# Shared-expert products in sixes instead of twelves through the last unit of cross-attention

## The chip, the cores and the metric

The kernel runs on one core of one Trainium2 chip. The metric is the device time of one execution, in microseconds (us), lower being better. Engines are named as the profile names them: PE (matrix multiply; PEld is its weight load), DVE (vector), ACT (activation), POOL, and SP, which issues most of the loads. TensorE's granted clock is given as a share of full speed.

## The reference, cut to what matters

One pre-norm decoder layer on `x` of 16 sequences by 64 tokens by 256 features (1024 tokens), all in float32:

```
x = x + self_attention(layernorm(x))          # 16 heads, weights as 4-bit codes times scales
x = x + cross_attention(layernorm(x), ctx)    # 16 heads, context of 64 rows by 64
x = x + moe(layernorm(x))

def moe(xt):                                  # 16 experts of inner width 176, plus shared experts of 352
    scores  = softmax(xt @ Wg.T)              # the 4 best of 16 experts, out of the 2 best groups of 4
    y       = sum over chosen experts of w_e * (silu(xt @ W1_e.T) * (xt @ W3_e.T)) @ W2_e.T
    z       = (silu(xt @ Ws1.T) * (xt @ Ws3.T)) @ Ws2.T
    return y + z
```

In cross-attention each head's normalized scores are multiplied with the context, then projected back to 256 features and added to `x`. The products `xt @ Ws1.T` and `xt @ Ws3.T` are the "shared up products" of this document.

## The kernel before, in words

Tokens lie on the 128 partitions in eight tiles of 128 (`x[0]` to `x[7]`), handled as two halves of 512 tokens. A float32 product is made from two rounded parts of each operand, a high and a low one: `three` lists the three part products, so that a 256-deep product of one tile is six matmuls. `parts_of` (L111) makes the parts: ACT copies the high part, DVE subtracts to get the low one (both rows stand under L112 and L113).

Cross-attention runs in eight units, each four heads (a "quad") of one half. In turn n of the loop the unit n is rotated, unit n-1 is scored and unit n-2 finished. To finish a unit means: `transposed` (L352) turns the normalized scores `pn` on PE, ACT copies the result into `pt` in two rows (L360, L361), `pair_context` (L1070) multiplies `pt` with the context into PSUM tile `av`, `parts_of` turns `av` into `c_t`, and `cross_project` (L1095 for its additions) projects four tiles of 128 tokens with 24 matmuls and lets DVE add them to `x`. Each unit has two pairs of heads, so two `pn`, two `pt`, two `c_t`.

Turn 9 finishes the last unit, of the second half of the tokens. Nothing of cross-attention is left to be mixed in, so the shared up products of the first half (`normed[0]`, ready since turn 6) stand there: six products of six matmuls, called in pairs by `shared_up` (two products and the Silu on ACT, L937), each followed by `shared_hidden` (DVE multiplies gate and up, L948, and splits the result in parts) and later by `shared_output` (36 matmuls, additions L970).

After the last projection the second half is normalized (`layernorm_t(3, (1,))`: statistics on DVE, one power on POOL L177, two rows of ACT L199 and two of DVE L192), turned on PE (L216), and routed by `choose(1)`: 16 small matmuls with the router's weights, a long run of small DVE instructions (L791 to L856), and in their midst two matmuls L819 and L820 for the places in the experts' lists. Its last row (L856) gives the targets of the 16 indirect transfers by which POOL scatters the tokens to the experts (`send`, L864). The experts' loop loads its inputs `xr` from there (L1311).

The builder's scheduler decides the order within each engine from estimated times. `after(...)` (a wrapper of `tc.issue_after`) is the author's way to hold an instruction's place behind another one in that order; it adds no wait on the chip. PSUM has four `mm` tiles, two `at` and two `av`. SP loads the last expert's weights in two pieces (`dense_weights`: `w_last_up`, `w_last_down`), and then the weights of the experts 0 and 1 (L277), which wait until the last `pn` has been computed.

Of the kernel before, what the change touches and what calls it, by code (L numbers as in the profile page):

```python
# [44 lines left out]
SHI = 2 * INTER  # L45
# [26 lines left out]
def decoder_layer(ctx: ExitStack, tc: tile.TileContext, a: dict, out: bass.AP):  # L72
    nc = tc.nc
# [11 lines left out]
    def mm_tile(rows=128, cols=512):  # L85
        return ps_mm.tile([128, 512], F32, tag="mm", name="mm")[:rows, :cols]
# [15 lines left out]
    def matmuls(ps, pairs):  # L102
        for n, (l, r) in enumerate(pairs):
            m = nc.tensor.matmul(ps, lhsT=l, rhs=r, start=(n == 0), stop=(n == len(pairs) - 1))  # L104
        return m.ins

    def three(left, right):

        return [(left[0], right[0]), (left[0], right[1]), (left[1], right[0])]

    def parts_of(src, hi, lo, eng=None):  # L111
        nc.scalar.copy(hi, src)  # L112
        return (eng or nc.vector).tensor_tensor(lo, src, hi, ALU.subtract).ins  # L113


    x_pairs = [acts.tile([128, 2, D], F32, tag=f"x{n}", name=f"x{n}") for n in range(NI // 2)]
# [198 lines left out]
    with ExitStack() as attn:  # L315
# [603 lines left out]
            nc.vector.tensor_reduce(w, ch, AX.X, ALU.add)  # L919
            return w, last, p  # L920

        def shared_up(half, k, pool):

            n = min(128, SHI - k * 128)
            cols = slice(k * 128, k * 128 + n)
            ps = []
            for w in range(2):
                t = mm_tile(rows=n)
                pairs = []
                for c in range(2):  # L930
                    pairs += three(
                        [p[:, w, c, cols] for p in ws13_p], [p[:, c, :] for p in normed[half]]
                    )
# [3 lines left out]
            silus.append(nc.scalar.activation(g, ps[0], AF.Silu).ins)  # L937
# [43 lines left out]
        with (  # L981
# [179 lines left out]
            for n in range(len(units) + 2):  # L1161
# [7 lines left out]
                with after(*([projected] if n < len(units) and projected else [])):  # L1169
                    pts_n = [transposed(pn) for pn in pns.pop(n - 2, ())]  # L1170
                if n < len(units):
                    roped_done = list(roped_last)
                    order = [m for m in [next(rotate, None)] if m]
                    if n - 1 in here:
                        with after(*order, *([pn_turned[0]] if n > 2 else [])):
                            q_rs, product = pair_queries(
                                weights[units[n - 1][0]][1], roped.pop(n - 1), roped_done
                            )
                        order = [product]
                    c_ts = []  # L1180
                    for pt in pts_n:
                        with after(*order):
                            c_t, product = pair_context(pt, units[n - 2][1])
                        order = [product]
                        c_ts.append(c_t)
                    if n == 0:
                        with tc.issue_after(highs[-1]), tc.issue_after(lows[-1]):
                            xn_t += layernorm_t(2, (1,))
                    else:
                        pns[n - 1] = []  # L1190
                        for q_r in q_rs:
                            with after(*order):
                                pn, product = pair_scores(q_r, units[n - 1][1], nc.gpsimd)
                            order = [product]
                            pns[n - 1].append(pn)
                    if n in late:
                        with after(*order):
                            next(prep)
                    with after(*order):
                        next(rotate)  # L1200
                    if n in late:
                        next(prep)
                else:
                    if n - 1 in here:
                        q_rs, _ = pair_queries(weights[units[n - 1][0]][1], roped.pop(n - 1))
                    c_ts = [pair_context(pt, units[n - 2][1])[0] for pt in pts_n]
                    if n - 1 in here:

                        pns[n - 1] = [pair_scores(q_rs[0], units[n - 1][1], nc.vector)[0]]
                    if n - 1 in here:  # L1210
                        pns[n - 1].append(pair_scores(q_rs[1], units[n - 1][1], nc.vector)[0])
                if n - 2 in here:
                    projected = cross_project(
                        weights[units[n - 2][0]][2], c_ts, units[n - 2][1], n - 1 == len(units)
                    )
                for _ in rotate:
                    pass

# [23 lines left out]
                    choose(0)  # L1242
                    send(0, (0, 1))
                if n == 8:
                    w_last = dense_weights()
                    with after(exps[-1]):
                        routed.append(weights_of_choices(0))
                if n == 9:
                    rows[1] = [
                        xw.tile([128, 3, 2, 2, DC], F32, tag="w_s", name="rows1")  # L1250
                        .rearrange("p a b c d -> p (a b c d)")[:, : 2 * ROW]
                        .rearrange("p (a b) -> p a b", a=2)
                        for _ in range(2)
                    ]
                    normed[1] = layernorm_t(3, (1,), token_rows(1))[0]
                    high = highs[-1]
                    scored, placed, aimed = choose(1)
# [319 lines left out]
```

## Time and profile before

| What | Value |
|---|---|
| Time of four runs | 568.45, 572.49, 566.48, 569.26 us; median 568.85 |
| Profiled execution | 568.07 us; span 566.3 us |
| Mean granted clock of TensorE | 0.978 |
| PE / PEld busy | 528.0 / 446.8 us (93% / 79% of the span) |
| DVE / ACT / POOL busy | 385.2 / 304.1 / 227.6 us |
| Turn 9 on PE (from the last unit's first transposes to the second half's transposes) | 392.4 to 417.7 us |
| Routing of the second half (first router matmul to targets) | 419.1 to 430.8 us |
| Scatter of the second half on POOL | from 431.1 us |

A row of a timeline gives the start in us, the time from the first instruction's start to the last one's end, the engine, the line, the operation, what it writes and reads, the shape and the number of instructions; in brackets stands how long the engine was idle before it and what released it. Rows of PE are pipelined: the next row starts before the last one's end, so a stretch is best measured from start to start.

### The profile page before, as it was taken

Reading aid. Unit: us, or ns where it says so; the run is one execution under the profiler, and the core shown is the slowest. Engines: PE = TensorE matmul, PEld = TensorE weight load, DVE = VectorE, ACT = ScalarE, POOL = GpSimd, SP = SyncE. Lnnn points to the kernel's source line nnn. Section 1 sums busy time; section 2 is a strip of 40 time slices with the busy share of each in tenths; the row PEclk is TensorE's granted clock in tenths of the full one; section 3 lists DMA queues with packets and bytes.
Section 4 is the critical chain, followed back from the end, with each engine's and each line's share of the span. In section 5 each row is a group of like instructions: output and inputs, shape, how many; then the busy total and the mean of one; then the engine's idle time right before and its main releaser. Section 6 shows DMA issues by size and latency. Waiting matters only on the chain.

```text
span 566.3 us, 10815 instructions
## 1 busy us (share of the span) xinstructions
PE 528.0 (93%) x4013; PEld 446.8 (79%) x4013; DVE 385.2 (68%) x863; ACT 304.1 (54%) x764; POOL 227.6 (40%) x213
## 2 busy tenths in 40 slices
PE   7999999999999989999999999999799679999972
PEld 6888898998989865867768678678587579999961
DVE  5465473664745899746566487677477489999877
ACT  3667566585575521534625455456426178777551
POOL 4261500101100017426333364453255716888862
PEclk9999999999999999999999999999899889999985
DMA  8464432823200889280010000102311648677475
GB/s 235 143 163 121 114 116 67 225 93 113 76 1 12 271 226 293 92 251 1 19 54 2 8 0 1 30 2 55 137 61 69 220 168 291 223 254 236 124 266 171
DMA packets 44263, 70.84 MB, mean 125 GB/s; under 512 B 11824, under 2 KB 25232, under 8 KB 44208
## 3 DMA queue, kind: packets, MB, share of 16 engines
q1 hardware_dynamic: 39376, 58.71, 35.4%
q0 software_dynamic: 3696, 10.36, 4.7%
q10 hardware_dynamic: 1136, 1.05, 0.5%
q8 instruction: 33, 0.54, 0.4%
q14 instruction: 22, 0.18, 0.1%
HBM read 48.61 MB, written 21.86 MB: 124 GB/s over the span
## 4 chain that ended last, share of the span: by engine, by line


## 5 line engine op out<-in xcount | busy, mean ns | idle before, releaser
L1014 POOL TENSOR_TENSOR roped<-rt,rt 128x512 f32<-128x512 f32 x48 | 61.8, 1309 | 44.9 <-DVE rt L1006 43.9
L104 PE MATMUL mm<-xn,w_q 128*128 128x512 f32 x288 | 72.3, 402 | 0.5 <-ACT xn L222 0.5
L1006 DVE TENSOR_TENSOR rt<-mm,rope_q 128x512 f32<-128x512 f32 x96 | 60.9, 679 | 11.5 <-PE mm L104 11.1
L104 PEld LDWEIGHTS mm<-xn,w_q 128*128 128x128 f32 x288 | 52.7, 188 | 14.4 <-issue 1.2
L104 PE MATMUL mm<-xs,w 128*128 128x384 f32 x270 | 55.0, 353 | 8.1 <-ACT xs L112 6.9
L1360 POOL DMA_INDIRECT yd<-y,to x45 | 48.1, 1068 | 27.0 <-ACT y L1355 13.4
L104 PEld LDWEIGHTS mm<-xs,w 128*128 128x128 f32 x270 | 48.3, 198 | 9.6 <-ACT xs L112 7.6
L325 DVE TENSOR_REDUCE sm_m<-at 128x8 f32<-128x512 f32 x32 | 21.9, 684 | 47.8 <-PE at L582 47.1
L523 POOL TENSOR_TENSOR wv<-code,scale 128x512 fp32r<-128x512 f32 x7 | 9.5, 1352 | 89.7 <-DMA scale<-in_scales 55.6
L1032 PE MATMUL mm<-roped,w_s 128*64 128x512 f32 x192 | 44.9, 599 | 0.2 <-DVE rt L1006 0.2
L331 ACT ACTIVATE p<-at,sm_m 128x64 f32<-128x64 f32 x128 | 38.1, 346 | 12.7 <-DVE sm_m L329 12.6
L565 ACT ACTIVATE qT<-mm,bqkv 128x512 f32<-128x512 f32 x32 | 21.8, 689 | 33.6 <-PE mm L104 33.6
L360 ACT COPY pt<-at 64x512 f32<-64x512 f32 x32 | 18.6, 581 | 38.7 <-PE at L352 38.7
L104 PE MATMUL av<-w,hp 128*128 128x256 f32 x225 | 35.6, 292 | 1.8 <-ACT y L1355 0.9
L104 PE MATMUL mm<-wv,xn 128*128 128x256 f32 x256 | 36.2, 288 | 0.0
L104 PE MATMUL mm<-wo,o 128*128 128x256 f32 x256 | 34.1, 286 | 2.0 <-DVE x L624 1.8
L343 POOL TENSOR_TENSOR pn<-p,sm_s 128x512 f32<-128x512 f32 x14 | 14.6, 1044 | 50.1 <-DVE sm_s L339 50.1
L104 PEld LDWEIGHTS mm<-wo,o 128*128 128x128 f32 x256 | 31.6, 191 | 3.6 <-DVE x L624 3.1
L104 PE MATMUL mm<-xn,wk 128*128 128x512 f32 x128 | 34.3, 399 | 0.0
L104 PE MATMUL mm<-xn,wq 128*128 128x512 f32 x128 | 33.2, 398 | 0.1
L104 PEld LDWEIGHTS av<-w,hp 128*128 128x128 f32 x225 | 30.7, 191 | 3.0 <-ACT y L1355 1.5
L104 PEld LDWEIGHTS mm<-wv,xn 128*128 128x128 f32 x256 | 32.5, 189 | 0.7
(219 smaller groups left out, 1189.9 us busy)
## 6 DMA issues: line engine op xcount, KB each, us to landing
w<-in_W SPq DMA_DIRECT2D x15, 640.0 KB
code<-in_codes SPq DMA_DIRECT2D x32, 256.0 KB
scale<-in_scales SPq DMA_DIRECT2D x32, 256.0 KB
xr<-xd SPq DMA_DIRECT2D x15, 408.0 KB
xd<-zeros SPq DMA_DIRECT2D x8, 720.0 KB
yd<-zeros SPq DMA_DIRECT2D x8, 512.0 KB
got<-yd SPq DMA_DIRECT2D x16, 256.0 KB
wq<-in_Wq SPq DMA_DIRECT2D x4, 512.0 KB
```

The lines of the kernel that those rows point to most:

```text
L104: m = nc.tensor.matmul(ps, lhsT=l, rhs=r, start=(n == 0), stop=(n == len(pairs) - 1))
L325: nc.vector.tensor_reduce(m, sc, AX.X, ALU.max)
L331: last = nc.scalar.activation(p[:, b], sc[:, b], AF.Exp, bias=m[:, b : b + 1], accum_out=s[:, b : b + 1])
L343: .tensor_tensor(pn, p, s.unsqueeze(2).broadcast_to(shape), ALU.mult)
L360: nc.scalar.copy(pt[:S, :, 0, :], ps[:S])
L523: mults[n] = eng.tensor_tensor(w, *loaded[gr].pop(n), ALU.mult).ins
L565: nc.scalar.activation(qk[which][:, half * 512 : (half + 1) * 512], ps, AF.Identity, bias=bqkv[:, which, h : h + 1],).ins
L1006: factors = nc.vector.tensor_tensor(mt, ps3, rope_table(t, 2 * ab + k), ALU.mult)
L1014: nc.gpsimd.tensor_tensor(r.rearrange("p (b s) -> p b s", s=S), one, two, op)
L1032: nc.tensor.matmul(ps[h // 2][(h % 2) * 64 : (h % 2) * 64 + 64], lhsT=w_s[:, t, blk, ab, :], rhs=roped[2 * t + ab], start=first[h], stop=l ...
L1360: sent = nc.gpsimd.indirect_dma_start(out=yd[: (E - 1) * SLOTS + min(TOPK, E - 1 - e) * NT], out_offset=bass.IndirectOffsetOnAxis(ap=to[:, ...
```

## The change

In turn 9 the finishing of the last unit is written out by hand. A helper `shared_products` makes one product of six matmuls. The order on PE becomes: transposes of the first pair, one product, context of the first pair, transposes of the second pair, one product, context of the second pair, one product, then the whole projection (24 matmuls) in one piece, and the other three products behind it. Before, two products (twelve matmuls) stood in each of the two gaps, and the last two products stood inside the projection. The Silus and what follows them are ordered behind the high part of the second `c_t`. The split of `w_last_down` into parts, which stood ahead of the first `c_t` on ACT, is put behind the second `c_t` on ACT and DVE. The count of instructions on each engine is the same. In the built order the transposes of the second half (L216) come after 18 of the 36 matmuls of `shared_output`, no longer after all, and the first six matmuls of `dense_up` come behind the router's matmuls instead of ahead of them.

```diff
     def parts_of(src, hi, lo, eng=None):
-        nc.scalar.copy(hi, src)
+        high_last[0] = nc.scalar.copy(hi, src).ins
         return (eng or nc.vector).tensor_tensor(lo, src, hi, ALU.subtract).ins
...
-        def shared_up(half, k, pool):
+        def shared_products(half, k, w):
 
             n = min(128, SHI - k * 128)
             cols = slice(k * 128, k * 128 + n)
-            ps = []
-            for w in range(2):
-                t = mm_tile(rows=n)
-                ...
-                matmuls(t, pairs)
-                ps.append(t)
+            t = mm_tile(rows=n)
+            pairs = []
+            for c in range(2):
+                pairs += three([p[:, w, c, cols] for p in ws13_p], [p[:, c, :] for p in normed[half]])
+            return t, matmuls(t, pairs)
+
+        def shared_up(half, k, pool, ps=None):
+
+            n = min(128, SHI - k * 128)
+            ps = ps or [shared_products(half, k, w)[0] for w in range(2)]
...
                     nc.sync.dma_start(out=t, in_=a["W123"][E - 1][:, cols])
-                    parts_of(t, parts[0][:, cols], parts[1][:, cols])
-                return parts
+                    if cols.start == 0:
+                        parts_of(t, parts[0][:, cols], parts[1][:, cols])
+                return parts, lambda: parts_of(t, parts[0][:, cols], parts[1][:, cols])
...
+                if n == len(units) + 1:
+
+                    half, ups, c_ts, order = units[-1][1], [], [], []
+                    for pn in pns.pop(n - 2):
+                        with after(*order):
+                            pt = transposed(pn)
+                        with after(pn_turned[0]):
+                            ps, product = shared_products(0, 0, len(ups))
+                        ups.append(ps)
+                        with after(product):
+                            c_t, product = pair_context(pt, half)
+                        c_ts.append(c_t)
+                        order = [product]
+                    c_high = high_last[0]
+                    with after(product):
+                        ps, product = shared_products(0, 1, 0)
+                    ups.append(ps)
+                    with after(product):
+                        projected = cross_project(weights[units[-1][0]][2], c_ts, half, True)
+                    with after(c_high):
+                        rest_of_last()
+                else:
...
                     for k in range(3):
-                        with after(*pn_turned[(0 if k else 1) :]):
-                            up = shared_up(0, k, xa)
+                        while len(ups) < 2 * k + 2:
+                            with after(projected):
+                                ups.append(shared_products(0, k, len(ups) % 2)[0])
+                        with after(c_high):
+                            up = shared_up(0, k, xa, ups[2 * k : 2 * k + 2])
```

More of the change, by code (lines that the diff above doesn't have):

```diff
@@ L111, in parts_of @@
     def parts_of(src, hi, lo, eng=None):
-        nc.scalar.copy(hi, src)
+        high_last[0] = nc.scalar.copy(hi, src).ins
         return (eng or nc.vector).tensor_tensor(lo, src, hi, ALU.subtract).ins
+    high_last = [None]
     x_pairs = [acts.tile([128, 2, D], F32, tag=f"x{n}", name=f"x{n}") for n in range(NI // 2)]
@@ L920, in weights_of_choices @@
             return w, last, p
-        def shared_up(half, k, pool):
+        def shared_products(half, k, w):
             n = min(128, SHI - k * 128)
             cols = slice(k * 128, k * 128 + n)
-            ps = []
-            for w in range(2):
-                t = mm_tile(rows=n)
[L929 to L933, printed above, removed]
-                matmuls(t, pairs)
-                ps.append(t)
+            t = mm_tile(rows=n)
[6 more added lines that the diff above has]
+            ps = ps or [shared_products(half, k, w)[0] for w in range(2)]
             g = pool.tile([128, 512], F32, tag=f"rt{k % 2}0", name="sg")[:n]
@@ L1168, in decoder_layer @@
                 rotate = iter(rotated_queries(weights[qd][0], half, roped[n]) if n in here else ())
[L1169 to L1178, printed above, removed]
-                        order = [product]
-                    c_ts = []
-                    for pt in pts_n:
-                        with after(*order):
[L1183 to L1188, printed above, removed]
-                    else:
[L1190 to L1215, printed above, removed]
+                if n == len(units) + 1:
[9 more added lines that the diff above has]
+                        c_ts.append(c_t)
+                        order = [product]
+                    c_high = high_last[0]
[7 more added lines that the diff above has]
+                else:
+                    with after(*([projected] if n < len(units) and projected else [])):
+                        pts_n = [transposed(pn) for pn in pns.pop(n - 2, ())]
+                    if n < len(units):
+                        roped_done = list(roped_last)
+                        order = [m for m in [next(rotate, None)] if m]
+                        if n - 1 in here:
+                            with after(*order, *([pn_turned[0]] if n > 2 else [])):
+                                q_rs, product = pair_queries(
+                                    weights[units[n - 1][0]][1], roped.pop(n - 1), roped_done
+                                )
+                            order = [product]
+                        c_ts = []
+                        for pt in pts_n:
+                            with after(*order):
+                                c_t, product = pair_context(pt, units[n - 2][1])
+                            order = [product]
+                            c_ts.append(c_t)
+                        if n == 0:
+                            with tc.issue_after(highs[-1]), tc.issue_after(lows[-1]):
+                                xn_t += layernorm_t(2, (1,))
+                        else:
+                            pns[n - 1] = []
+                            for q_r in q_rs:
+                                with after(*order):
+                                    pn, product = pair_scores(q_r, units[n - 1][1], nc.gpsimd)
+                                order = [product]
+                                pns[n - 1].append(pn)
+                        if n in late:
+                            with after(*order):
+                                next(prep)
+                        with after(*order):
+                            next(rotate)
+                        if n in late:
+                            next(prep)
+                    else:
+                        if n - 1 in here:
+                            q_rs, _ = pair_queries(weights[units[n - 1][0]][1], roped.pop(n - 1))
+                        c_ts = [pair_context(pt, units[n - 2][1])[0] for pt in pts_n]
+                        if n - 1 in here:
+                            pns[n - 1] = [pair_scores(q_rs[0], units[n - 1][1], nc.vector)[0]]
+                        if n - 1 in here:
+                            pns[n - 1].append(pair_scores(q_rs[1], units[n - 1][1], nc.vector)[0])
+                    if n - 2 in here:
+                        projected = cross_project(
+                            weights[units[n - 2][0]][2], c_ts, units[n - 2][1], n - 1 == len(units)
+                        )
@@ L1244, in decoder_layer @@
                 if n == 8:
-                    w_last = dense_weights()
+                    w_last, rest_of_last = dense_weights()
                     with after(exps[-1]):
```

## The prediction

> **What bounds the kernel now.** I read the page first: one engine is nearly always busy, so what counts is where PE stops, and what it waits for there.
>
> ```profile
> span 566.3 us, 10815 instructions
> PE 528.0 (93%) x4013; PEld 446.8 (79%) x4013; DVE 385.2 (68%) x863; ACT 304.1 (54%) x764; POOL 227.6 (40%) x213
> ```
>
> The change touches turn 9 alone, so next comes the timeline of PE there.
>
> ```profile
> 392.73 3.05 PE L104 MATMUL mm<-xn,ws 128*128 128x512 f32 x12
> 395.71 1.09 PE L1070 MATMUL av<-pt,kv 128*64 128x128 f32 x16
> 396.73 0.65 PE L352 MATMUL at<-ident,pn 128*128 128x128 f32 x4
> 397.14 3.05 PE L104 MATMUL mm<-xn,ws 128*128 128x512 f32 x12
> 404.01 1.34 PE L1070 MATMUL av<-pt,kv 128*64 128x128 f32 x16 [3.82 <-ACT pt L361]
> 405.27 1.01 PE L104 MATMUL av<-w_o,c_t 128*128 128x256 f32 x3
> 406.08 3.88 PE L104 MATMUL mm<-xn,ws 128*96 128x512 f32 x12
> 409.80 3.03 PE L104 MATMUL av<-w_o,c_t 128*128 128x256 f32 x21
> 412.67 4.37 PE L104 MATMUL mm<-ws,sh 128*128 128x256 f32 x36
> ...
> 419.14 2.17 PE L104 MATMUL av<-wg_p,xn 128*128 128x32 f32 x16
> 421.16 3.04 PE L104 MATMUL mm<-xn,w_last 128*128 128x512 f32 x12
> 424.05 2.96 PE L104 MATMUL mm<-xn,ws 128*128 128x512 f32 x12
> 427.80 0.41 PE L819 MATMUL av<-sel,upto 128*128 128x64 f32 x2 [0.79 <-DVE sel L762]
> ```
>
> PE stops once, 3.82 us before the second context product, because ACT delivers the second `pt` late. Why late, the timeline of ACT tells:
>
> ```profile
> 395.61 0.62 ACT L112 CAST w_last<-w_last_down 128x512 fp32r<-128x512 f32 x1 [1.43 <-DMA w_last_down<-in_W]
> 402.29 0.58 ACT L112 CAST c_t<-av 128x512 fp32r<-128x512 f32 x1 [6.06 <-remote]
> 402.77 0.58 ACT L360 COPY pt<-at 64x512 f32<-64x512 f32 x1
> 403.37 0.58 ACT L361 COPY pt<-at 64x512 f32<-64x512 f32 x1
> 403.97 1.28 ACT L937 ACT_TABLE_LOAD   x1
> ```
>
> The copy `c_t` waits in the program for one thing, the first context product, whose row on PE ends at 396.80. It starts 5.5 us later, and the view names no one. The `pt` stands behind it on ACT. I call this the hold. While it lasts, SP's two weight loads (issued at 394.62) and POOL's first eight scatters are moving. The table by stretches shows both that traffic and what the stop does to the clock:
>
> ```profile
> 396.00:404.00 8.00, 4.19 (x32) 3.12 (x28) 2.66 (x7) 1.90 (x5) 3.83 (x4) 1.00 0.74 249
> 404.00:408.20 4.20, 4.19 (x25) 3.15 (x26) 2.14 (x4) 3.85 (x6) 0.00 (x0) 0.59 0.00 1
> ```
>
> The columns are PE, PEld, DVE, ACT, POOL, granted clock, DMA share and GB/s: DMA is 0.74 busy during the hold, and the clock 0.59 after the stop.
>
> Last, what hangs on turn 9: POOL's scatter of the second half, idle until the targets are there.
>
> ```profile
> 431.10 1.16 POOL L864 DMA_INDIRECT xd<-rows,to  x1 [5.26 <-DVE to L856]
> ```
>
> Experts 0 to 3 need these transfers one group of four after another, and PE is busy only 11.2 of the 17 us from 443 to 460. So the end of turn 9 and the routing behind it set when the experts' stage begins; a us gained there should come through.
>
> **The change part by part.** Matmuls, copies and transfers are as many as before on every engine; only places move. SP's and POOL's queues are in the old order, and all that SP's weight loads wait for lies before the change, so this traffic again starts at 394.62.
>
> *Removed: the stop and its slow clock.* 3.82 us, and the rows behind it, from start to start: 16 context matmuls 1.26 us against 1.02 in the first pair, three projection matmuls 0.81 against 0.37 (21 take 2.87, a projection of 24 elsewhere 2.97, so 0.124 each), twelve products 3.72 against 2.98. That is 0.24 + 0.44 + 0.74 = 1.4 us. Together 5.2 us.
>
> *The new order on PE, if nothing is held.* Six products take half of 2.98, 1.49 us. So the first context product runs at 394.22 to 395.24, its `pt` being done at 394.18; the transposes follow to 395.65, six products to 397.14. ACT now has no `w_last` copy ahead: `c_t` at about 395.5 to 396.1, `pt` at 396.1 to 397.3. The second context product starts at 397.3 (0.2 us of idle PE) and ends at 398.35, six products at 399.84.
>
> *A new wait.* The projection uses two `av` buffers, so its third tile waits for DVE's addition of the first. That addition now stands behind `sgh` (L948) on DVE, `sgh` behind the Silu on ACT, and the Silu behind the second `c_t`, the moved `w_last` copy and the table load: 398.6 + 0.6 + 0.6 + 1.28 + 0.55 + 0.7 + 0.4 = 402.8. PE has done two tiles at 401.33, and stands 1.5 us. Before, twelve products inside the projection covered this. Queued behind the wait on PE are all later products, and on DVE the statistics of the normalization. The rest of the projection ends at 404.3.
>
> *What now stands behind the projection* covers the normalization: six products (1.49) and twelve narrower ones (2.98 at full clock) until 408.75, 18 of `shared_output` at 4.20/36 = 0.117 until 410.85, transposes 0.8, 18 more, and 413.75 is reached. The rows that the transposes need come at about 409.6 (ACT does one Silu first, until 408.5), and the router's operands at 413.7: no wait. Router matmuls: 413.75 + 2.02 = 415.8, against 421.16. Gain 5.4 us, of which about 1.5 is the first six of `dense_up`, moved behind.
>
> *Routing.* PE needs 18 products of `dense_up` (4.36) and twelve more (2.9 to 3.0) to reach L819 at 423.1, against 427.80. DVE has its selection at 415.8 + 6.5 = 422.3 (427.65 - 421.16 = 6.5), so the 0.79 us of waiting go. L820 follows at 423.5 against 428.61, and the targets come 5.1 us earlier. POOL's third and fourth group of the first half wait for the last low part, at 411.2, and take 8 x 1.27 = 10.2 us, until 421.4: they don't hold the rest up.
>
> *The moved split of `w_last_down`* (0.62 us on ACT, 0.69 on DVE) is counted above in the new wait on ACT; DVE's is hidden by that wait too. If the wait went, it would cost up to 0.7 us there. The operand is used after 434, far off.
>
> *The sum.* PE's own line gains 5.2 - 0.2 - 1.5 = 3.5 us, and 1.2 from the waits at L819 and L820; the routing gains 5.1. What of it comes through I bound by 3.5 (PE's line alone) and 6.4 (5.1 plus 1.3, as DVE stood 1.3 us behind its own row at L762, which may or may not come back), and take 4.4, between the two lines that meet at the first `xr` transposes at 442.94. 568.07 - 4.4 = 563.7 for the profiled execution; its time is 0.8 under the median of the four runs, so 568.85 - 4.4 = 564.4.
>
> **A rule against it.** The row of a matmul ends at 396.80, and its reader starts at 402.29. The Trainium skill (Perfetto Trace Analysis, Per-engine timelines) says that a matmul's end in the profile is an estimate, and that the real release comes after PSUM's acknowledgement and the semaphore's way, which no row shows. By the rows, the first copies of the new order are free at 395.5 and the sum is the one above. By the rule, the release has a duration of its own that no row measures and that an earlier matmul need not shorten, and the sum would be that of the second or third case below. No row settles it.
>
> **The rivals.** Nothing shows what the hold is. It lies between 393.0, when a copy still followed its transposes at once, and 402.3.
>
> *Held from the middle on.* For it speaks that the traffic is the same, at the same time. If PE's releases are stuck only from about 396 to 402.3, the first `c_t` and second `pt` (395.5, 395.9) get through, and the second context product's doesn't: `c_t` at 402.3 instead of 398.6, 3.7 us later, with all of the new wait behind it. 4.4 - 3.7 = 0.7 gained, less up to 0.8 if the clock falls again: 568.1 to 569.0, taken 568.3.
>
> *Held from the start.* If releases after 395 are stuck, `c_t` and `pt` come at 402.3 to 404.0 as before, but PE has only six products to do meanwhile instead of twelve. It stands from 397.1 to 404.0, 6.9 us, and does the six later. From 404.0: context 1.3, six products 1.8 on the slow clock, half a projection 1.6, a wait until 409.7, half a projection 1.5, 18 products 4.5, 36 matmuls 4.2, transposes 0.8, router 2.0 reach 422.7, 1.5 later than before, and L819 430.0, 2.2 later. 568.85 + 2.2 = 571.1. It decides as soon as the second `pt` starts later than about 400. This is the slower side. Against it: no release of PE falls due between 393.0 and 396.8 in the old order, so nothing shows that it began so early.
>
> *No effect:* if the stage of the experts were held by its weight loads alone, turn 9 would not matter, 568.9. Against it stands POOL's 5.26 us of waiting for targets.
>
> **How the numbers follow.** Not held: 0.43, 564.4, own range 562.4 to 565.4. Held from the middle: 0.28, 568.3. Held from the start: 0.22, 571.1. No effect: 0.07. One per cent, 5.7 us, is about what a measurement of this kernel can tell from no change. Only the upper part of the first case passes it, and I give that part half, since the routing line alone gains 5.1 and small waits behind it may go as well: 0.22. A slower one by over 1% needs the third case with another stop: 0.12. Within: 0.66. Range 561.8 to 571.6.
>
> **What would show it.** Right: the second context product starts near 397.3 with almost no idle time; `c_t` follows its matmuls at once; a wait of 1 to 2 us inside the projection for DVE's addition; granted clock 1.00 until 420; router matmuls done near 416, targets near 425.7, first `xr` transposes near 438. Wrong: an idle stretch of over 2 us ended by ACT anywhere between 395 and 405, or targets earlier by 5 us and the end not.

## The result, and the profile after

The changed kernel's profiled execution took 567.40 us (span 565.3), the kernel before 568.07 (566.3). Over all executions the medians are 576.27 us (41 runs, 567.40 to 580.28) against 568.39 (67 runs, 564.32 to 574.94). The ratio is 1.0039, 95% interval 1.0020 to 1.0058: slower by 0.4%, inside one per cent. Of the changed kernel's executions 13 lie from 567.4 to 571.2 and 28 from 572.4 to 580.3, and the ratio leaves out those over 1.5% above the fastest, so it is smaller than the 1.4% between the medians. The forecast, 564.4, was wrong in its direction.

The page of the kernel after is nearly that of before:

```profile
span 565.3 us, 10815 instructions
PE 528.6 (94%) x4013; PEld 447.3 (79%) x4013; DVE 386.0 (68%) x863; ACT 305.0 (54%) x764; POOL 228.6 (40%) x213
```

The timeline of PE in turn 9. In this execution turn 9 begins 1.48 us earlier than in the one of before (first transposes at 390.89, not 392.37), from noise ahead of it (390.2 to 393.4 over the profiles of this case, with either kernel); below, times behind "+" count from these transposes.

```profile
392.82 1.09 PE L1072 MATMUL av<-pt,kv 128*64 128x128 f32 x16
393.85 0.65 PE L354 MATMUL at<-ident,pn 128*128 128x128 f32 x4
394.26 1.65 PE L104 MATMUL mm<-xn,ws 128*128 128x512 f32 x6
399.98 1.18 PE L1072 MATMUL av<-pt,kv 128*64 128x128 f32 x16 [4.07 <-issue]
401.09 2.93 PE L104 MATMUL mm<-xn,ws 128*128 128x512 f32 x6
403.82 3.30 PE L104 MATMUL av<-w_o,c_t 128*128 128x256 f32 x24
406.95 4.34 PE L104 MATMUL mm<-xn,ws 128*128 128x512 f32 x18
...
425.77 0.41 PE L821 MATMUL av<-sel,upto 128*128 128x64 f32 x2 [0.67 <-PE mm L104]
426.57 0.43 PE L822 MATMUL av<-before,ones 128*128 128x64 f32 x2 [0.40 <-DVE before L817]
```

The six products, the context, the transposes and six more stand within 0.1 us of the prediction. Then PE stops again ahead of the second context product: 4.07 us, where it had been 3.82. "Issue" names no releaser, but the product starts 0.06 us after the second `pt` is done on ACT:

```profile
397.26 0.59 ACT L112 CAST c_t<-av 128x512 fp32r<-128x512 f32 x1 [4.56 <-issue]
398.74 0.58 ACT L362 COPY pt<-at 64x512 f32<-64x512 f32 x1 [0.90 <-remote]
399.34 0.58 ACT L363 COPY pt<-at 64x512 f32<-64x512 f32 x1
```

The first `c_t` needs the context product that ended at 393.91, and starts 3.35 us later. The hold is back, against a product that stands 1.4 us nearer to the start of the turn (+1.93, not +3.34). The table by stretches (PE, PEld, DVE, ACT, POOL, granted clock, DMA share, GB/s) shows the clock fall behind it as before:

```profile
396.00:404.00 8.00, 4.02 (x23) 3.18 (x24) 1.98 (x3) 4.52 (x7) 2.74 (x3) 0.80 0.56 206
404.00:408.20 4.20, 4.20 (x31) 3.95 (x30) 3.60 (x11) 1.32 (x3) 0.00 (x0) 0.97 0.00 0
```

From start to start the sixteen context matmuls take 1.11 us, the six products 2.73 and the projection 3.13. Where nothing is held (below) they take 1.03, 1.51 and, elsewhere, 2.97: 1.46 us for the slow clock, the 1.4 of before once more. And the targets are little earlier:

```profile
429.07 1.15 POOL L866 DMA_INDIRECT xd<-rows,to  x1 [5.07 <-DVE to L858]
```

That is +38.18 against +38.73, a gain of 0.55 us; at the first `xr` transposes +50.09 against +50.57; at the end of the span 174.4 against 173.9 us behind the first transposes. What little the turn gains, the experts' stage gives back.

### The profile page after: what moved, and what is told of

It reads as the page before. It is cut to its first block, busy times and chain, and to the rows that moved or that the text cites. A ratio compares the mean times of both kernels' runs of the same rounds, so it can differ in the third digit from the quotient of the medians.

```text
span 565.3 us, 10815 instructions
## 1 busy us (share of the span) xinstructions
PE 528.6 (94%) x4013; PEld 447.3 (79%) x4013; DVE 386.0 (68%) x863; ACT 305.0 (54%) x764; POOL 228.6 (40%) x213
## 4 chain that ended last, share of the span: by engine, by line
PE 76%; DVE 9%; issue 5%; ACT 4%; DMA 2%; POOL 2%; another core or an unknown queue 2%; DVEq 0%; ACTq 0%; POOLq 0%; SPq 0%
PE mm L104 42%; PE mm L1034 8%; PE av L603 4%; PE av L104 4%; PE at L584 3%; PE at L354 3%; PE av L1072 3%; PE at L1059 2%; DVE rt L1008 2%; PE at L1349 1%; PE mm L464 1%; POOL yd L1388 1%; PE mm L442 1%; DMA yd<-y,to 1%
```

## The experiments

Two theories were set against each other. **The hold**: something in turn 9's traffic holds PE's releases back, and with six products between the steps PE has less to do meanwhile than with twelve. **The order**: the loss comes from the projection in one piece, with its wait for DVE, or from the moved split, and not from the hold.

The runs came to different chips, and this became the finding that mattered. Each run was compared with the kernel before on its own chip. On three chips that kernel takes 554 to 555 us (the *free* chips below), on two others 568 us, as at first (the *held* chips); the chip of the first result is not on record. Each chip was used in one call of the runs alone, so that the chip makes the difference, and not something else about the call, is likely but not shown. The times in the expectations were written before this was known; idle times and ratios are what to compare.

### On a free chip: traffic moved away

```diff
-        nc.sync.dma_start(out=t, in_=src)                # weight_parts, experts 0 and 1
+        load = nc.sync.dma_start(out=t, in_=src).ins
+        behind(load, [projected])                        # the last matmul of the projection
```

This edit is `a_late_w` on the changed kernel, `b_late_w` on the kernel before; the order on every engine stays.

> The changed kernel, with one edit: SP's loads of the weights of experts 0 and 1 wait for the last matmul of the cross-attention's projection; the order on every engine is as before the edit. If these loads are what holds PE's releases back, the first c_t follows its context product within 1 us, the second context product starts with less than 0.5 us of idle PE (4.07 us now), the router's matmuls end near 414 (417.9 now) and the time is 564 to 566 us, with no execution above 571. If the hold comes from something else (the scatters, or the order of the instructions), the idle 4 us stay and the time is that of the changed kernel, 569 to 580; the late loads themselves should cost nothing, since the weights are read after 430.

> The kernel before, with the same edit. If the loads hold the releases back, the stop of 3.82 us ahead of the second context product shrinks below 0.5 us and the slow clock behind it goes: 568.4 - 5.2 = 563 us, so that the kernel before without its hold is about as fast as the changed one without it. If the hold is of another source, 3.8 us of stop and 568 us.

`a_late_s` moves the call `send(0, (0, 1))`, POOL's first eight scatters, from turn 7 to behind the projection; `a_late_ws` has both edits.

> The changed kernel, with POOL's first eight scatters (choices 0 and 1 of the first half) behind the projection instead of ahead of turn 9; the weight loads are where they were. If the scatters are needed for the hold, the idle time ahead of the second context product falls below 0.5 us; if the weight loads alone make it, 3 to 5 us remain. The scatters then follow one another from 407 to about 428, just ahead of those of the second half (429), so their lateness should cost 0 to 2 us.

> The changed kernel with both edits: neither the weight loads nor the scatters move during turn 9. If either kind of traffic, or the two together, is the cause, there is no idle stretch of over 0.5 us between 393 and 400. If 3 to 5 us remain, the cause is in the order of the instructions and not in the traffic. Time 564 to 568 in the first case.

Measured against the kernel before on the same chip: `a_late_w` 1.0026 (1.0008 to 1.0045), `b_late_w` 1.0003 (0.9982 to 1.0024), `a_late_s` 1.0120 (1.0084 to 1.0157), `a_late_ws` 1.0165 (1.0130 to 1.0200). In none of the four profiles is there a stop ahead of the second context product. That looked like an answer, but `a_late_s` had the loads where they were and no stop, so a control was due. The late scatters are themselves dear: POOL issues sixteen in a row and goes straight on with those of the second half, and the first `xr` transposes wait 6.30 us for their load (5.74 in `a_late_ws`); 0 to 2 us had been expected.

### On another free chip: the controls, and parts of the change undone

> The kernel before, unchanged, with a profile from the chip of this call. If the hold belongs to the traffic of the weight loads and the scatters together, its 3 to 4 us of idle PE ahead of the second context product are there; with the loads moved away (the earlier run) there was none. If they are missing here too, the hold comes and goes from chip to chip, and the earlier run with late loads showed nothing of the loads.

> The changed kernel, unchanged, on the same chip. If the hold decides: 4 us or more of idle PE ahead of the second context product and executions 3 to 10 us above those with late loads. If no hold is there: the idle time goes, the wait of 1.2 us for DVE's addition inside the projection appears as in the run with late loads, and the time is 0 to 2 us above the kernel before, since then the change has nothing to gain.

The kernel before took 554.94 us, the changed one 557.26: 1.0032 (1.0009 to 1.0054), by its size the loss of the first result, though, as the rows show, made in another way. And neither has a hold, with loads and scatters in their old places. The runs with moved traffic had shown nothing of the hold. The timeline of PE for the changed kernel here:

```profile
397.46 1.09 PE L1072 MATMUL av<-pt,kv 128*64 128x128 f32 x16
398.49 1.67 PE L104 MATMUL mm<-xn,ws 128*128 128x512 f32 x6
400.00 1.58 PE L104 MATMUL av<-w_o,c_t 128*128 128x256 f32 x12
402.80 1.69 PE L104 MATMUL av<-w_o,c_t 128*128 128x256 f32 x12 [1.22 <-DVE x L1097]
404.33 4.33 PE L104 MATMUL mm<-xn,ws 128*128 128x512 f32 x18
```

and for the kernel before:

```profile
398.56 1.09 PE L1070 MATMUL av<-pt,kv 128*64 128x128 f32 x16
399.59 0.62 PE L104 MATMUL av<-w_o,c_t 128*128 128x256 f32 x3
400.05 2.94 PE L104 MATMUL mm<-xn,ws 128*96 128x512 f32 x12
402.82 3.02 PE L104 MATMUL av<-w_o,c_t 128*128 128x256 f32 x21
```

Here PE never stops in the old order, so there is no stop to remove, and the new order adds the wait that was predicted: the projection's third tile stands 1.22 us for DVE's addition, which is queued behind `sgh` and the Silu. At L822 the changed kernel is at +29.96, the old one at L820 at +29.22: 0.74 us late, and 0.74 us it stays at the targets (+32.40 against +31.66) and at the first `xr` transposes (+42.66 against +41.92).

Two variants put parts of the change back. `a_12` has twelve products in each gap again, with the projection in one piece:

```diff
-                            ps, product = shared_products(0, 0, len(ups))
-                        ups.append(ps)
+                            for w in range(2):
+                                ps, product = shared_products(0, len(c_ts), w)
+                                ups.append(ps)
...
-                    with after(product):
-                        ps, product = shared_products(0, 1, 0)
-                    ups.append(ps)
```

> The changed kernel with twelve products in each of the two gaps, as before the change, and only the last twelve behind the projection, which stays in one piece. If the number of products that cover the hold is what costs, the idle time ahead of the second context product is 1.5 to 3 us shorter than in the changed kernel and the time is 1 to 6 us lower. If the one-piece projection and its wait for DVE's addition are the cost, the time is that of the changed kernel within 1 us, and the wait of 1 to 1.5 us stays.

`a_rest` puts the split of `w_last_down` back ahead of the first `c_t` (`rest_of_last()` is called at once in turn 8).

> The changed kernel with the split of w_last_down back where it was, ahead of the c_t copies on ACT and DVE. If the split's new place is part of the wait inside the projection (0.62 us on ACT and 0.69 on DVE ahead of sgh), the wait falls from 1.2 to about 0.5 us and the time by up to 0.7 us; the first c_t comes up to 1.3 us later, which twelve products would hide and six do not: 0 to 1 us of idle PE ahead of the second context product. Within 1 us of the changed kernel either way.

Measured: `a_12` 1.0041 (1.0014 to 1.0069), `a_rest` 1.0031 (1.0008 to 1.0054). Neither wins any time back. The projection of `a_12`:

```profile
401.53 1.09 PE L104 MATMUL av<-w_o,c_t 128*128 128x256 f32 x7 [0.23 <-DVE c_t L113]
404.36 1.95 PE L104 MATMUL av<-w_o,c_t 128*128 128x256 f32 x12 [1.74 <-DVE x L1097]
```

and of `a_rest`:

```profile
396.17 1.09 PE L1072 MATMUL av<-pt,kv 128*64 128x128 f32 x16 [0.48 <-ACT pt L363]
400.98 0.97 PE L104 MATMUL av<-w_o,c_t 128*128 128x256 f32 x6 [0.70 <-DVE x L1097]
402.37 0.98 PE L104 MATMUL av<-w_o,c_t 128*128 128x256 f32 x6 [0.41 <-DVE x L1097]
```

With twelve the wait is longer, not shorter (0.23 + 1.74), and the clock falls behind it (0.76 and 0.81; the columns are those of the table above):

```profile
404.00:408.00 4.00, 3.64 (x17) 2.89 (x18) 4.00 (x11) 1.24 (x2) 0.00 (x0) 0.76 0.00 0
408.00:412.00 4.00, 4.00 (x23) 3.15 (x22) 1.52 (x7) 1.16 (x2) 0.44 (x1) 0.81 0.00 0
```

Its targets come at +35.90, 4.24 us later than in the kernel before; at the end of the span 2.3 of them are left. With the split moved back the wait of 1.22 was expected to fall to 0.5; instead it goes to other places and grows: 0.48 ahead of the context, 0.70 and 0.41 in the projection, with the targets at +33.10. On this chip the changed kernel stops in turn 9 at the projection alone.

### On a third free chip: the wait taken away, and a hold put in

`a_in` moves one group of six products into the projection, behind its first two tiles; `a_sgh` orders DVE's first `sgh` behind the first two additions.

```diff
     # a_in: in cross_project
+                    if k == 2 and between:
+                        order = [between(m)]             # shared_products(0, 1, 1)
     # a_sgh: in the block of turn 9
-                            hs.append(shared_hidden(k, *up, xa, part))
+                        with after(c_high, *([] if k else added[-3:-2])):
+                            hs.append(shared_hidden(k, *up, xa, part))
```

> The changed kernel with one of its groups of six products moved from behind the projection to its middle, after the first two tiles. Where nothing is held, the wait of 1.2 us for DVE's addition lies under these six (1.49 us): no idle PE in the projection, the targets 0.7 to 1.2 us earlier than in the changed kernel, and the time level with the kernel before or up to 0.5 us below it (1.8 us below the changed one). If the loss of the changed kernel has another source, its time does not move.

> The changed kernel with DVE's first sgh product put behind the additions of the projection's first two tiles. The third tile then waits no longer for the Silu's chain: the wait of 1.2 us inside the projection falls below 0.3 us, and the time falls by about 1 us, level with the kernel before. If the wait is hidden anyway, the time stays that of the changed kernel.

Measured: `a_in` 1.0017 (0.9994 to 1.0039), `a_sgh` 1.0004 (0.9985 to 1.0023), where the changed kernel, on the chip before, had 1.0032; the intervals overlap, so the rows must decide. In `a_sgh` the projection runs through, and the targets are at +31.51, against +31.66 in the kernel before and +32.40 in the changed one:

```profile
398.99 3.15 PE L104 MATMUL av<-w_o,c_t 128*128 128x256 f32 x24
```

In `a_in` the six cover the wait (400.23 to 401.62), the targets come at +31.90, 0.5 us earlier than in the changed kernel where 0.7 to 1.2 had been expected. So without a hold the wait for DVE's addition makes the whole delay of the targets. Neither version beats the kernel before: both are level with it.

`a_hold5` and `b_hold5` make a hold: the first `c_t` on ACT also waits for POOL's sixth scatter to land (`behind(copied, [sent_rows[5]])`), and the second `pt` stays behind it. In the kernel before the turn's first lines are written out for this; PE's order stays.

> The changed kernel with an artificial hold: the copy of the first c_t on ACT also waits for the sixth of POOL's scatters to land (about 9.7 us after turn 9's first transposes, as late as the hold of the first profile of the kernel before, 9.9), and the second pt stays behind it. If six products cover too little, PE stands 6 us or more ahead of the second context product (it arrives 4.9 us after the first transposes, the pt is there at 11.3), the clock falls behind it, and the time rises by 5 to 8 us against the same kernel without the hold, to 562 to 565 us where that has 557. If a stop in turn 9 is given back behind it, by the waits for DVE and the routing that it covers, the rise is under 3 us.

> The kernel before with the same artificial hold. PE arrives at the second context product 7.7 us after the first transposes, so it stands about 3.6 us, and with the slow clock 5 us are lost: 555 + 4 to 5 = 559 to 560 us. If the cover decides, this is 3 to 5 us less than the changed kernel with the same hold; if not, the two differ by 1 to 2.5 us, as without a hold.

The changed kernel took 563.50 us, 1.0176 (1.0151 to 1.0200); the kernel before 559.79, 1.0125 (1.0092 to 1.0158). Both expectations held. The second context product of each:

```profile
403.39 1.98 PE L1073 MATMUL av<-pt,kv 128*64 128x128 f32 x16 [6.89 <-ACT pt L364]
```

```profile
402.50 1.95 PE L1071 MATMUL av<-pt,kv 128*64 128x128 f32 x16 [4.01 <-ACT pt L362]
```

For nearly the same hold (the `pt` done at +11.85 and +11.78) PE stands 2.88 us longer in the changed kernel, about the 2.98 us of products that the two gaps have given away. The targets come at +40.23 against +37.33. With a hold the change costs 2.9 us up to there, without one 0.74.

### On a held chip

> The changed kernel, unchanged, once more. If this chip holds PE's releases back as in the first profiles, the second context product stands 4 us or more and the executions reach from 567 to 580; if it does not, the projection shows its wait of 1.2 us and the time is 555 to 558 us, 0.3% above the kernel before. A chip between these would speak against the hold as something that a chip has or has not.

> The changed kernel with the weight loads of experts 0 and 1 behind the projection, once more, beside the unchanged one. Where the hold is there, this tells its cause: if the loads make it, the idle 4 us go and the time falls by 4 us or more; if not, they stay. Where no hold is there, both kernels are within 1 us of each other.

The kernel before took 568.30 us here, the changed one 576.51, 1.0127 (1.0084 to 1.0170), and with late loads 578.43, 1.0181 (1.0142 to 1.0220). PE in the changed kernel:

```profile
401.41 1.98 PE L1072 MATMUL av<-pt,kv 128*64 128x128 f32 x16 [6.21 <-ACT pt L363]
...
443.56 1.22 PE L104 MATMUL mm<-ws,sh 96*128 96x256 f32 x4 [3.26 <-issue]
...
454.48 6.19 PE L104 MATMUL mm<-xs,w 128*128 128x384 f32 x18 [8.42 <-ACT xs L112]
```

the last of these rows in the first profile of the kernel before:

```profile
446.22 4.70 PE L104 MATMUL mm<-xs,w 128*128 128x384 f32 x18 [2.47 <-ACT xs L112]
```

and with late loads, its second context product and the table's row for the stop:

```profile
401.16 1.98 PE L1073 MATMUL av<-pt,kv 128*64 128x128 f32 x16 [5.53 <-ACT pt L364]
```

```profile
398.00:402.00 4.00, 0.84 (x8) 0.84 (x10) 0.69 (x1) 1.48 (x3) 0.96 (x1) 0.71 0.19 70
```

The stop remains with the loads gone and the DMA engines 0.19 busy. A full DMA does not make the hold. The rows of the changed kernel show a second thing: two more stops, while POOL scatters the second half. The one at 454.48 was 2.47 us in the first profile of before and 2.44 in that of after, and is 8.42 here; the one at 443.56 was 1.61 and 1.67, and is 3.26. Behind the first transposes this execution needs 184.4 us where the first profile of before needs 173.9. Of the 10.5 us, 1.7 are there at the targets (+40.45), 3.8 at the first `xr` transposes, and the other 6.7 come with the stop at 454.48, 5.95 us longer, and the slow clock behind it (its eighteen matmuls take 6.03 us from start to start, against 4.54). That is how a time of 576 arises.

`a_hold3` and `b_hold3`, on the same chip, made the first `c_t` wait for the fourth scatter.

> The changed kernel with a shorter artificial hold: the first c_t waits for the fourth scatter to land, 6 to 9 us after the first transposes. With 7.5 us, the second pt is there at 9.1, PE arrives at 4.9 and stands 4.2 us, as in the first profile of the changed kernel (4.07); less the wait of 1.0 us that goes in the projection, and with up to 1.4 us of slow clock, the time is 3 to 5 us above the kernel before, plus the 0.7 us that the change costs anyway: 558 to 561.

> The kernel before with the same shorter hold. PE arrives at 7.7 us and stands 1.4 us at most, too little for the clock to fall: 0 to 1.5 us above the kernel before, 555 to 556. If the cover by twelve products is what the change gives up, the two kernels are again 3 to 5 us apart.

They tell little of a short hold, since this chip's own was longer: in `b_hold3` the copy's releaser is again unnamed, and PE stood 3.88 us; in `a_hold3` 6.24 us, the last 0.23 of it by the chip's hold. Both expectations missed. The ratios are 1.0003 (0.9960 to 1.0046) for `b_hold3` and 1.0019 (0.9962 to 1.0077) for `a_hold3`, but the executions scatter: four of six of `a_hold3` took 579 to 581 us, and two of six of `b_hold3` 577 and 579.

### On another held chip: the scatters moved away

In four profiles with a hold, the last ACT row that PE's late releases let go starts 1.48 to 1.57 us after the end of POOL's last scatter of the turn (402.29 behind 400.81 in the kernel before, 400.17 behind 398.64 in the changed one on the held chip, and `a_hold3` and `b_hold3`); with late loads it is 0.85, and in the first profile of after that row starts 0.60 us ahead of that end. In the changed kernel on the held chip:

```profile
397.68 0.96 POOL L866 DMA_INDIRECT xd<-wkq,to  x1 [0.30 <-issue]
```

```profile
397.31 0.59 ACT L112 CAST c_t<-av 128x512 fp32r<-128x512 f32 x1 [5.32 <-remote]
400.17 0.58 ACT L362 COPY pt<-at 64x512 f32<-64x512 f32 x1 [2.27 <-remote]
```

The Trainium skill (Perfetto Trace Analysis, Per-engine timelines) says that such a row on POOL ends when the last descriptor has been made, not when the data has moved. By it the hold would go with the making of descriptors; no run here separates that from the moving of the data. To see whether the scatters make the hold at all, the two kernels with late scatters were run again, on a chip where the kernel before takes 568 us:

> The changed kernel with POOL's first eight scatters behind the projection, once more, for a chip that has the hold. There the weight loads alone could be moved without effect, and in three of four held profiles PE's last late release came 1.45 to 1.48 us after the last of these scatters had left POOL. If the scatters make the hold, the first c_t follows its product within 1.3 us and the second context product starts with less than 0.5 us of idle PE. If not, 4 to 6 us of idle PE stay. Where there is no hold at all, 0 us and 1.2% above the kernel before, as the first time.

> The changed kernel with weight loads and scatters both behind the projection, once more, for a chip that has the hold. If 4 to 6 us of idle PE stay even here, neither traffic makes the hold, and PE's releases are late there by themselves; if they go here and not with the scatters alone moved, either kind of traffic is enough for it.

`a_late_s` took 578.41 us here, 1.0188 (1.0132 to 1.0244), `a_late_ws` 577.80, 1.0133 (1.0086 to 1.0179); the kernel before 568.32. PE in `a_late_s`:

```profile
398.05 1.09 PE L1072 MATMUL av<-pt,kv 128*64 128x128 f32 x16
...
403.39 1.69 PE L104 MATMUL av<-w_o,c_t 128*128 128x256 f32 x12 [1.22 <-DVE x L1097]
...
420.10 1.56 PE L104 MATMUL mm<-xn,ws 128*128 128x512 f32 x6
430.90 2.93 PE L104 MATMUL mm<-xn,ws 128*128 128x512 f32 x6 [9.24 <-issue]
```

With the scatters gone, turn 9 runs to the tenth of a us as on a free chip (the second context product at +4.95, there +4.94): no stop, and the wait of 1.22 us in the projection, though the loads move in it. And the hold has gone where the scatters went. POOL's first and last of the sixteen, and ACT's copies ahead of and behind them:

```profile
408.78 1.21 POOL L866 DMA_INDIRECT xd<-wq,to  x1 [0.20 <-issue]
...
428.05 0.96 POOL L866 DMA_INDIRECT xd<-wkq,to  x1 [0.31 <-issue]
```

```profile
396.18 0.59 ACT L112 CAST c_t<-av 128x512 fp32r<-128x512 f32 x1 [1.26 <-PE av L1072]
...
430.25 0.60 ACT L1129 ACTIVATE dense<-mm 128x512 f32<-128x512 f32 x1 [17.19 <-remote]
```

The products that the copy at 430.25 waits for ended at about 417.3 (six of the row of eighteen from 415.81). Their release came 12.9 us later, 1.2 us after POOL's last scatter. On the free chip the same copy, in the same kernel, started at 416.64, in the midst of the scatters. PE stood 9.24 us; the same stop in `a_late_ws`, 8.44 us, names ACT's `dense` copy as its releaser, so PE seems to have been out of `mm` tiles. The unmoved kernels were not profiled on this chip; that it holds is seen from the stop at the new place. So POOL's run of scatters holds PE's releases back, on these chips and not on the free ones, and its stop came with it when it was moved.

## Why the prediction was wrong

**Where it failed.** The step is "Removed: the stop and its slow clock", with the case "not held" that carried it. The stop was taken as a property of PE's order, to be removed with it, 5.2 us. The prediction saw that the same traffic runs in both kernels, and still gave the case without a hold 0.43, because no row showed the hold before 396. The stop belongs to POOL's eight scatters, which the change leaves in their place. On a held chip it comes back (4.07, 6.21 us); on a free chip it was never there. The size of the term was right: between the first profile of the kernel before and the free one the stop and the slow rows behind it make 3.82 + 0.23 + 0.35 + 0.95 = 5.35 us, and the waits at L819 and L820 (0.79 and 0.40) are gone there as well. But this is what the hold costs, not what the order costs: the forecast needed a hold before and none after, and no pair of profiles showed that.

**The rival that came.** "Held from the start" was priced 571.1 us, with PE idle for 6.9 us and L819 2.2 us late. The ratio of 1.0039 on 568.85 is 571.1 too, but this agreement is in part luck: the medians are 1.4% apart, and on the chip of the later pair, where all six executions took 572 to 579 us, 1.0127 is past it. The idle time was 4.07 in the first profile, 6.21 in the later one and 6.89 with the artificial hold; the targets were 0.55 us early, 1.7 late, and 2.9 later than with the old order under the same hold. The mechanism, six products covering too little, is shown by the artificial hold. The case did not have the longer stop at the experts' first inputs (8.42 us). It stands in all three profiles of the changed kernel and its variants on the later chip, at 577 to 580 us; that it makes the slower executions of the first result as well is likely, but none of them has a profile.

**The other steps.** The order on PE without a hold was right: the second context product at +4.93 was predicted, +4.94 measured. The new wait was sized 1.5 us; it is 1.22 on free chips, and 0 to 0.2 behind a hold, where the stop ahead of it swallows most of it (0.22 in `a_hold5`). The earlier router and routing (5.1 us) were counted against a held kernel before; against a free one the targets come 0.74 us later. The moved split, counted inside the wait, shows nothing in the time (`a_rest`: 1.0031 against 1.0032), though its targets come 0.7 us later with the split moved back. "No effect" is refuted: a later turn 9 did make a later end, in `a_hold5`.

**The rule weighed against it** was right in its kind. The release of a matmul does have a duration of its own that the rows don't show: on held chips, while POOL scatters, it was 3.35 to 12.9 us, and mostly lasted until about the end of POOL's run; on a free chip the first `c_t` started 0.05 us after its product's row.

**What is open:** why a run of scatters holds releases back on some chips and not on others, and why the stop at the experts' inputs is 2.4 us in some executions and 8.4 in others. In the three profiles with the short one (before, after, `b_hold3`: 2.44 to 2.47 us) one scatter's row on POOL, just ahead of it, takes 2.16 to 2.22 us, and DVE's first row on PE's products of that stage starts up to 0.2 us behind its end (444.21 behind 444.02 in before); that the two hang together is not shown; in the three with the long one (the changed kernel on the held chip, with late loads, `a_hold3`: 8.40 to 8.83 us) none of the sixteen takes over 1.5. The same three have the longer stop ahead of four matmuls as well (3.16 to 3.26 us of `issue`, where the first three have 1.61 to 1.67), which no run tested either.

## What to carry to other kernels

A stop belongs to what makes it, not to the place where it shows: before work is moved to fill it, or taken out of its cover, find the engine whose rows begin and end with it, and move that engine's work once, as a test: here the kernels with the scatters moved were 1.2 to 1.9% slower than the kernel before. Where the releaser is unnamed, keep the cover wide, for the twelve products hid 2.9 us more than the six. And a profile from one chip is one sample: the changed kernel stood for 4.07, 6.21 and 0 us at the same place in its three profiles.

## What the runs showed of the hardware

- **Scatters against releases.** On the held chips, while POOL issues a run of indirect transfers (one in 1.27 us), PE's releases to ACT and DVE, and, as it seems, DVE's to itself (a `remote` wait of 3.14 us ahead of a row that follows DVE's own), arrive up to 12.9 us late, most of them in a burst at or after the end of the run. Single ones get through on the way (the first `c_t` at 397.31 in the changed kernel, with scatters until 398.64), and the run does not hold from its first row on: in `a_late_s` ACT's copy at 411.99, 3.2 us behind the first scatter's start, still comes 0.86 us after the start of its transposes, as on the free chip. On the free chips the same programs show none of it.
- **Chips.** The kernel before takes 554 to 555 us on three chips and 568 on two, and 568 in the first result. Up to the first `xr` transposes it needs 41.9 and 50.6 us from turn 9's first transposes: 8.65 of the 14 us lie in this stretch, where POOL scatters.
- **The clock.** In the first two stretches of 2 us, counted from the start of the second context product, the granted clock was 0.50 to 0.72 in all eight profiles with a stop of 3.82 to 6.89 us ahead of that product, and 0.50 in both behind the stops of 5.53 us and more. In the third stretch it was 0.93 to 1.00 in five of them and 0.50 to 0.75 in three (`a_late_w_d`, `b_hold3`, `a_hold3`). After the stop of 6.21 us sixteen context matmuls took 1.90 us from start to start instead of 1.03. A stop of 1.22 us left the clock at 1.00, but the two of `a_12`, 0.23 and 1.74, were followed by 0.76 and 0.81 in the next two stretches of 4 us: its last twelve products took 4.34 us from start to start, against 2.77 for the same twelve in the free kernel before. Whether the second stop alone would have done that is not shown.
